# Layer norm in a four-layer network: the first transposition of a norm's tokens also waits for the last of the four normed tiles

## The chip, the cores and the metric

The kernel runs on one core of a Trainium2 chip, as one program with one launch. The metric is the device time in microseconds (us). Each kernel is run several times and the median counts. A profiled execution gives the trace from which the durations and waits below are read.

## The reference

Four layers are applied to `x` of shape (4, 64, 64, 128): four images of 4096 tokens with 128 channels, all in 32-bit floats.

```python
x = L0(x)   # LN -> in_proj -> depthwise 3x3 conv -> four selective scans over 4096 steps
            # (16 states for each of 256 channels) -> LN -> gate -> out_proj; then LN -> MLP
x = L1(x)   # attention over all 4096 positions, softmax over the queries' axis
x = L2(x)   # convolution blocks: 1x1, 3x3, hard swish
x = L3(x)   # LN -> 7x7 neighbourhood attention; then LN -> MLP

def _ln(x, w, b):
    mu = x.mean(-1, keepdims=True)
    var = ((x - mu) ** 2).mean(-1, keepdims=True)
    return (x - mu) * rsqrt(var + 1e-05) * w + b
```

The layer norm stands at four places: ahead of `in_proj` and ahead of the MLP in layer 0, ahead of the attention and ahead of the MLP in layer 3. (The norm ahead of the gate in layer 0 is done in another way and isn't touched.)

## The kernel before, in words

**Work and stages.** Every image goes through the same stages, in chunks of 512 tokens, eight to an image. `scan_inputs` (L283) makes what the scan reads. `selective_scan` (L463) does the recurrence: for each tile GpSimd multiplies `du` with the rows of B (L510, tile `dB`), ScalarE makes exp(delta * A) (L516, `dA`), VectorE scans along the tokens (L518), VectorE or GpSimd multiplies with the rows of C (L523, L531, `hc`), and TensorE sums over the states with a constant matrix `pick` (L564, `py`). `scan_output` (L590), layer 1, layer 2 and `layer3_attention` (L1277) follow; the program calls these together `rest` (L1693). Layer 3's MLP is mixed with the next image's `scan_output`, except for the last image, where `layer3_attention` runs it as `mlp_steps`.

**What runs beside what.** In `network` (L1723) the scan of an image is given a priority number from 10,000,000 on (L1762), and everything else has small numbers, counted up as the program is written. While image 0 is scanned, the `scan_inputs` of images 1 to 3 run in the gaps or ahead of it; while image n is scanned, `rest` of image n-1 runs. After the last scan only `rest` of image 3 is left, with the MLP of image 2 in its first part.

**Who sets the order.** The order of instructions on an engine is not the program's. The framework (`tile.TileContext(nc, schedule_with_timeline_sim=True)`, L1855) plans it when the kernel is built: it keeps its own clock with estimated durations, and at each point gives an engine the instruction with the smallest number among those whose inputs are there by that clock and for which a tile buffer is free. On the chip each engine's queue then has this planned order, and semaphores hold an instruction back where its data comes later than planned. `after` (L88) adds a wait that the data alone would not ask for; its uses in the kernel (L570, L875, L1402 and `Together`, L101) let the first matmul of a group wait for the last of the group's inputs.

**The norm.** `layernorm_T` (L184) handles four tiles of 128 tokens. VectorE makes the statistics (L194, L196), ScalarE the reciprocal deviation (L180, L181), its negative (L198) and four shifts (L200). Then, tile by tile, ScalarE writes the normed tile (L204, `ln_xn`) and TensorE transposes it into a quarter of one PSUM tile (L207). Last, ScalarE reads all four quarters, applies weight and bias, and writes `xnT` (L208), which the next matmuls read. Below, N0 to N3 are the four normed tiles and T0 to T3 the four transpositions. The norm is called 128 times: 32 each in `scan_inputs` (L346), `scan_output` (L662), the attention of layer 3 (L1358) and the MLP of layer 3 (L1315 or L1667). The PSUM tile comes from a pool with four banks in most places; with `wide` (the last image) the attention and the MLP share one buffer for it (L1297).

`everything_again` (L1705), which has further calls, is only run when a bound is exceeded, and the trace shows nothing of it.

Of the kernel before, what the change touches and what calls it, by code (L numbers as in the profile page):

```python
# [87 lines left out]
def after(tc, later, earlier, kind=mybir.DependencyClass.Sync):  # L88
    tc.add_manual_dep(
        later.ins, earlier.ins.name, mybir.DependencyInfo(kind, mybir.DependencyReason.DATA), reason="group"  # L90
    )
# [86 lines left out]
def rstd_of(nc, K, out, var):  # L178

    nc.scalar.activation(out, var, AF.Ln, bias=K.eps)  # L180
    nc.scalar.activation(out, out, AF.Exp, scale=-0.5)  # L181


def layernorm_T(tc, K, pool, psum, x, w, b, out):  # L184


    nc = tc.nc
    stats = pool.tile([128, 4, 6], F32, name="ln_stats", bufs=2)
    mv = pool.tile([128, 4, 2], F32, name="ln_mv", bufs=2)
    rstd = pool.tile([128, 4], F32, name="ln_rstd", bufs=2)  # L190
    less = pool.tile([128, 4], F32, name="ln_less", bufs=2)
    shift = pool.tile([128, 4], F32, name="ln_shift", bufs=2)
    for t in range(4):
        nc.vector.bn_stats(stats[:, t, :], x[:, t, :])  # L194
    for t in range(4):
        nc.vector.bn_aggr(mv[:, t, :], stats[:, t, :])  # L196
    rstd_of(nc, K, rstd, mv[:, :, 1])
    nc.scalar.activation(less, rstd, AF.Copy, scale=-1.0)  # L198
    for t in range(4):
        nc.scalar.activation(shift[:, t : t + 1], mv[:, t, 0:1], AF.Copy, scale=less[:, t : t + 1])  # L200
    xn = pool.tile([128, 4, 128], F32, name="ln_xn", bufs=1)
    pt = psum.tile([128, 4, 128], F32, name="ps")
    for t in range(4):
        nc.scalar.activation(  # L204
            xn[:, t, :], x[:, t, :], AF.Identity, bias=shift[:, t : t + 1], scale=rstd[:, t : t + 1]
        )
        nc.tensor.transpose(pt[:, t, :], xn[:, t, :], K.ident)  # L207
    nc.scalar.activation(out, pt.rearrange("p t c -> p (t c)"), AF.Identity, bias=b, scale=w)  # L208


# [72 lines left out]
def scan_inputs(tc, K, A, D, img):  # L283
# [5 lines left out]
    with ExitStack() as ctx:  # L289
# [50 lines left out]
        for c in range(NCH + 1):  # L340
            acts = []
            if c < NCH:
                xt = pool.tile([128, 4, 128], F32, name="x")
                nc.sync.dma_start(xt, token_tiles(A["x"][img], c))
                xnT = pool.tile([128, LC], F32, name="xnT")
                layernorm_T(tc, K, pool, psum, xt, ln_w, ln_b, xnT)  # L346
                band = pool.tile([128, ND, RC + 2, W], F32, name="band", bufs=3)
                bands[c] = band
                for d in range(ND):
                    ps = psum.tile([128, LC], F32, name="ps")  # L350
                    nc.tensor.matmul(ps, in_proj[:, d * 128 : (d + 1) * 128], xnT, start=True, stop=True)
                    rows = ps.rearrange("p (h w) -> p h w", w=W)
                    nc.scalar.copy(band[:, d, 1 : RC + 1, :], rows)
                    if c > 0:
                        nc.scalar.copy(bands[c - 1][:, d, RC + 1, :], rows[:, 0, :])
                        nc.scalar.copy(band[:, d, 0, :], bands[c - 1][:, d, RC, :])
                sz = pool.tile([128, ND, LC], F32, name="sz")
                for d in range(ND):
                    ps = psum.tile([128, LC], F32, name="ps")
                    mm = nc.tensor.matmul(  # L360
                        ps, in_proj[:, DI + d * 128 : DI + (d + 1) * 128], xnT, start=True, stop=True
                    )
                    if d == 0:
                        together.open(mm)
                    acts.append(lambda d=d, ps=ps, sz=sz: nc.scalar.activation(sz[:, d, :], ps, AF.Silu))
# [224 lines left out]
def scan_output(tc, K, A, D, img, xT, last, scan_over=None):  # L590
# [6 lines left out]
    with ExitStack() as ctx:  # L597
# [17 lines left out]
        def chunk(c, psum=psum, together=together):  # L615
# [44 lines left out]
            yield  # L660
            xnT = pool.tile([128, LC], F32, name="xnT")
            layernorm_T(tc, K, pool, psum, x, ln_w, ln_b, xnT)  # L662
            yield
            po = yield from mlp(tc, K, P, pool, psum, together, xnT, x)
# [612 lines left out]
def layer3_attention(tc, K, A, D, img, wide, out=None):  # L1277
# [7 lines left out]
    with ExitStack() as ctx:  # L1285
# [27 lines left out]
        def mlp_steps(c, x):  # L1313
            xnT = pool.tile([128, LC], F32, name="xnT2", bufs=1)
            layernorm_T(tc, K, pool, made_in, x, n2_w, n2_b, xnT)  # L1315
            yield
            hT = pool.tile([128, NF, LC], F32, name="mlp_h", bufs=1)
            ph = psum.tile([128, NF, LC], F32, name="pair", tag="ps")
            for f in range(NF):
                mm = nc.tensor.matmul(ph[:, f, :], P.w1[:, span(f, 128)], xnT, start=True, stop=True)  # L1320
                if f == 0:
                    together.open(mm)
            together.run(
                mm,
                [
                    lambda f=f: nc.scalar.activation(hT[:, f, :], ph[:, f, :], AF.Gelu, bias=P.b1[:, f : f + 1])  # L1326
                    for f in range(NF)
                ],
            )
            yield  # L1330
            po = fresh((128, LC))
            for f in range(NF):
                nc.tensor.matmul(po, P.w2[:, f, :], hT[:, f, :], start=(f == 0), stop=(f == NF - 1))  # L1333
            yT = pool.tile([128, LC], F32, name="yT", bufs=1)
            nc.scalar.activation(yT, po, AF.Identity, bias=P.b2)  # L1335
            pt = fresh((128, 4, 128))
            for t in range(4):
                nc.tensor.transpose(pt[:, t, :], yT[:, span(t, 128)], K.ident)  # L1338
            nc.vector.tensor_add(x, x, pt)  # L1339
            nc.sync.dma_start(token_tiles(out, c), x)  # L1340
            yield
# [517 lines left out]
```

## Time and profile before

| what | value |
|---|---|
| median of 3 runs | 8721.23 us (8714.47 to 8724.86) |
| the profiled execution | 8724.62 us, its span 8722.7 us, 1.9 us around it |
| TensorE matmuls busy | 7011.5 us (80%) |
| VectorE busy | 7102.0 us (81%) |
| ScalarE busy | 5678.8 us (65%) |
| GpSimd busy | 7121.9 us (82%) |
| mean granted TensorE clock | 0.864 |

The span has three parts. Until about 2000 us the scan of image 0 runs beside `scan_inputs`. From there to about 7700 us the scans of images 1 to 3 run beside `rest` of images 0 to 2. From 7700 us on GpSimd does next to nothing, and `rest` of image 3 runs alone.

How to read the lines: a group's line has the line of the kernel, the engine, the operation, the tiles (output, arrow, inputs), the number of instructions, then busy time and mean duration, then idle time of the engine just ahead of them with what ended it. PE is TensorE's matmuls (a transposition is one), PEld its weight loads, DVE is VectorE, ACT ScalarE, POOL GpSimd, SP SyncE. In a timeline a row has start, duration, engine, line, operation, tiles, count and, in brackets, the idle time ahead of it and who ended it.

### The profile page before, as it was taken

How to read it: one execution, taken by the hardware profiler on the slowest of the kernel's cores; microseconds unless marked ns; L12 is line 12 of the kernel's file. 1: busy time of each engine (PE TensorE's matmuls, PEld its weight loads, DVE VectorE, ACT ScalarE, POOL GpSimd, SP SyncE). 2: the span in 40 equal slices, each digit the busy share in tenths (PEclk: the TensorE clock that was granted, in tenths of full speed). 3: DMA queues.
4: the chain of work that ended last, by engine and by line, in shares of the span. 5: the costliest groups of instructions: out<-in, count | busy, mean ns of one | idle time of the engine just before them, and what ended most of it. 6: DMA issues, size and time to landing. Idle time of an engine off the chain costs nothing. (4 is left out here: it accounts for less than half of the span.)

```text
span 8722.7 us, 102005 instructions
## 1 busy us (share of the span) xinstructions
PE 7011.5 (80%) x30532; PEld 2619.6 (30%) x30532; DVE 7102.0 (81%) x8456; ACT 5678.8 (65%) x11633; POOL 7121.9 (82%) x3111
## 2 busy tenths in 40 slices
PE   6858677686789987777899887777898877888988
PEld 2213122232422222233322222234322222344333
DVE  4788777778999999998899999998899999923433
ACT  5657676665666676667766676667766766654366
POOL 6899989999899989998899989998899999900000
PEclk8768687786899988888899988888999988899989
DMA  5676767677555556565555565565545565620020
GB/s 177 238 256 239 249 224 252 230 246 237 177 175 170 168 170 222 187 222 188 164 174 169 177 202 190 196 224 178 169 167 167 177 211 193 208 73 5 1 83 12
DMA packets 859600, 1562.74 MB, mean 179 GB/s; under 512 B 224389, under 2 KB 342300, under 8 KB 856733
## 3 DMA queue, kind: packets, MB, share of 16 engines
q1 hardware_dynamic: 728733, 1379.93, 48.2%
q10 hardware_dynamic: 130304, 176.19, 5.7%
q8 instruction: 245, 4.01, 0.2%
q14 instruction: 318, 2.61, 0.1%
HBM read 1286.50 MB, written 281.92 MB: 180 GB/s over the span
## 5 line engine op out<-in xcount | busy, mean ns | idle before, releaser
L510 POOL TENSOR_TENSOR dB<-du,b_rows 128x1024 f32<-128x1024 f32 x2048 | 4816.6, 2386 | 405.8 <-DVE hc L518 125.7
L516 ACT ACTIVATE dA<-dt,w_A_log 128x512 f32<-128x512 f32 x4096 | 2777.4, 690 | 482.3 <-DVE hc L518 257.7
L518 DVE TENSOR_TENSOR_SCAN dA<-dA,state,dB 128x512 f32<-128x512 f32 x2072 | 2563.4, 1274 | 289.8 <-POOL dB L510 151.8
L518 DVE TENSOR_TENSOR_SCAN hc<-dA,state,dB 128x512 f32<-128x512 f32 x1512 | 1874.1, 1270 | 303.3 <-ACT dA L516 114.2
L531 POOL TENSOR_TENSOR hc<-hc,c_rows 128x1024 f32<-128x1024 f32 x864 | 2061.9, 2386 | 60.6 <-ACT state L527 18.5
L523 DVE TENSOR_TENSOR hc<-dA,c_rows 128x512 f32<-128x512 f32 x2368 | 1526.0, 678 | 37.8 <-DMA c_rows<-bc_dram 15.2
L564 PE MATMUL py<-hc,pick 128*32 128x512 f32 x8192 | 1242.0, 681 | 266.6 <-POOL hc L531 230.9
L525 ACT COPY state<-dA 128x1 f32<-128x1 f32 x2072 | 319.2, 158 | 1225.5 <-DVE hc L523 1208.6
L854 PE MATMUL pa<-e,l_v 128*128 128x512 f32 x2048 | 1069.4, 654 | 14.9 <-ACT e L810 14.8
L810 ACT ACTIVATE e<-pair 128x1024 f32<-128x1024 f32 (+1 forms) x448 | 509.0, 1136 | 241.3 <-PE pair L806 233.7
L806 PE MATMUL pair<-l_g,l_f 32*128 32x512 f32 x2048 | 527.3, 662 | 169.6 <-ACT e L810 135.4
L854 PEld LDWEIGHTS pa<-e,l_v 128*128 128x128 f32 x2048 | 376.6, 200 | 667.1 <-issue 621.8
L994 POOL MEMSET l_h<- 64x128 f32 x8 | 1.9, 238 | 693.7 <-DVE l_h L968 693.7
L564 PEld LDWEIGHTS py<-hc,pick 128*32 128x32 f32 x8192 | 214.8, 116 | 1019.5 <-issue 476.1
L253 PE MATMUL ps<-band,w_conv_diag 128*128 128x504 f32 (+3 forms) x1152 | 499.0, 592 | 0.0
L1376 PE MATMUL pair<-table,ident 128*128 128x512 f32 x768 | 404.7, 652 | 104.2 <-ACT e L1386 68.7
L207 PE MATMUL ps<-ident,ln_xn 128*128 128x128 f32 x512 | 141.6, 375 | 377.4 <-ACT ln_xn L204 301.1
L518 DVE TENSOR_TENSOR_SCAN dA<-dA,dB 128x512 f32<-128x512 f32 x296 | 348.3, 1212 | 52.5 <-ACT dA L516 28.0
L334 POOL TENSOR_TENSOR du<-delta,xc 128x1024 f32<-128x1024 f32 x128 | 333.5, 2611 | 49.5 <-ACT delta L403 45.1
L1386 ACT ACTIVATE e<-pair 128x1024 f32<-128x1024 f32 (+1 forms) x224 | 254.3, 1135 | 101.4 <-PE pair L1380 100.7
L253 PEld LDWEIGHTS ps<-band,w_conv_diag 128*128 128x128 f32 x1152 | 220.3, 192 | 278.3 <-issue 259.7
L806 PEld LDWEIGHTS pair<-l_g,l_f 32*128 32x128 f32 x2048 | 138.4, 187 | 518.6 <-ACT e L810 266.9
(285 smaller groups left out, 8716.7 us busy)
## 6 DMA issues: line engine op xcount, KB each, us to landing
b_rows<-bc_dram SPq DMA_DIRECT2D x1024, 256.0 KB
c_rows<-bc_dram SPq DMA_DIRECT2D x1024, 256.0 KB
dt<-delta_dram SPq DMA_DIRECT2D x512, 512.0 KB
du<-du_dram SPq DMA_DIRECT2D x512, 512.0 KB
delta_dram<-delta ACTq DMA_DIRECT2D x128, 512.0 KB
du_dram<-du SPq DMA_DIRECT2D x128, 512.0 KB
table<-biasT_dram SPq DMA_DIRECT2D x72, 512.0 KB
y_first_dram<-y_sum ACTq DMA_DIRECT2D x128, 256.0 KB
```

Source lines behind the costliest of these rows:

```text
L253: mm = nc.tensor.matmul(out[:, r0 - row0 : r1 - row0, c0:c1], lhsT((dy + 1) * 3 + dx + 1), src[:, r0 + dy : r1 + dy, c0 + dx : c1 + dx], s ...
L334: nc.gpsimd.tensor_mul(du.rearrange("p d (a b) -> p d a b", b=H), deltas[b].rearrange("p d (a b) -> p d a b", b=H), tk,)
L510: nc.gpsimd.tensor_mul(dB, dus[pp], mid(bt, 2))
L516: nc.scalar.activation(dA, dts[pp][:, g, :], AF.Exp, scale=S.A[:, k, j, pr, g : g + 1])
L518: nc.vector.tensor_tensor_scan(hg[:, order], dA[:, order], dB[:, g, order], 0.0 if i == 0 else state[:, j, pr, g : g + 1], ALU.mult, ALU.add,)
L523: mm = nc.vector.tensor_mul(hc[:, g, :], dA, ct)
L531: made.append(nc.gpsimd.tensor_mul(hc, hc, mid(ct, 2)))
L564: mm = nc.tensor.matmul(py[0][32 * q : 32 * q + 32, :], S.pick, hcs[q // 2][:, q % 2, :], start=(k == 1 and j == 0), stop=(j == NJS - 1),)
L806: nc.tensor.matmul(ps[:, u, :], f[quad, t // 4, span(t % 4, 128)], g[quad, c, :], start=True, stop=True)
L810: made = nc.scalar.activation(e, ps, AF.Exp)
L854: nc.tensor.matmul(pa, v[:, 8 * q + t, :], es[q], start=(t == 0 and q == 0), stop=(t == 7 and q == 3),)
L1376: nc.tensor.matmul(ps[:, u, :], K.ident, t[:, u, :], start=True, stop=False)
```

## The change

The loop that normed a tile and transposed it becomes two loops: first all four normed tiles, then all four transpositions. T0 gets an added wait for N3, the last normed tile. No instruction is added or removed, and the arithmetic is the same. All four call sites get it.

```diff
     xn = pool.tile([128, 4, 128], F32, name="ln_xn", bufs=1)
     pt = psum.tile([128, 4, 128], F32, name="ps")
     for t in range(4):
-        nc.scalar.activation(
+        normed = nc.scalar.activation(
             xn[:, t, :], x[:, t, :], AF.Identity, bias=shift[:, t : t + 1], scale=rstd[:, t : t + 1]
         )
-        nc.tensor.transpose(pt[:, t, :], xn[:, t, :], K.ident)
+    for t in range(4):
+        turned = nc.tensor.transpose(pt[:, t, :], xn[:, t, :], K.ident)
+        if t == 0:
+            after(tc, turned, normed)
     nc.scalar.activation(out, pt.rearrange("p t c -> p (t c)"), AF.Identity, bias=b, scale=w)
```

## The prediction

> **What bounds the kernel now.** I read five views: the busy time by stretches, the waits of VectorE and GpSimd, the instructions on the tile `ln_xn`, the timeline around single norms, and the chain that ended last. First the stretches (length; busy us and count of PE, PEld, DVE, ACT, POOL; granted clock, DMA share, GB/s):
>
> ```profile
> 0.00:2000.00 2000.00, 1427.71 (x4420) 500.28 (x4420) 1493.55 (x1786) 1305.42 (x2953) 1775.62 (x795) 0.77 0.69 236
> 2000.00:7700.00 5700.00, 4696.83 (x21744) 1715.78 (x21745) 5257.22 (x6135) 3818.51 (x7856) 5345.48 (x2313) 0.88 0.57 186
> 7700.00:7920.00 220.00, 192.66 (x754) 111.76 (x753) 40.84 (x166) 145.98 (x301) 0.00 (x0) 0.95 0.15 45
> 7920.00:8420.00 500.00, 452.61 (x1761) 177.71 (x1760) 204.86 (x192) 205.12 (x198) 0.80 (x4) 0.96 0.04 11
> 8420.00:8722.70 302.70, 241.66 (x1856) 114.07 (x1856) 105.50 (x178) 203.73 (x329) 0.00 (x0) 0.90 0.14 51
> ```
>
> Up to 7700 us GpSimd is the bound: 7121.1 of 7700 us, idle 578.9, with VectorE close by (92% from 2000 us on) and TensorE at 82%. Behind 7700 us TensorE is: 886.9 of 1022.7 us, idle 135.8. So a wait of TensorE counts fully in the last part, and before it only where VectorE or GpSimd then wait for TensorE. Those waits, up to 7700 us (engine, line, releaser: us, times, longest):
>
> ```profile
> DVE hc L518 <- PE py L564: 122.3, 30, 11.2
> ...
> POOL dB L510 <- DVE hc L518: 125.7, 59, 8.1
> POOL dB L510 <- PE py L564: 53.2, 14, 9.2
> ```
>
> The tile that the change touches, over the whole span (who TensorE waited for ahead of T0 to T3, then who waited for them):
>
> ```profile
> L207 PE MATMUL ps<-ident,ln_xn x512: 272/421/477, 20.7 to 8701.6; 128*128 128x128 f32 x171
> ...
>   ACT ln_xn L204: 656.6, 189
> ...
>   ACT xnT L208: 22.5, 17
> ...
>   POOL hc L531: 7.7, 3
>   POOL dB L510: 2.2, 3
> ```
>
> 656.6 us counts the weight loads and the matmuls of the same stalls; by the matmul rows alone it is 301.1 (74 gaps over 1 us ahead of a transposition, of all releasers, sum to 369). Does the scan pay for it? I took every idle stretch over 1 us of VectorE or GpSimd up to 7700 us that TensorE ended (253 us together) and looked whether a gap over 1 us ahead of T0 lay in the 18 us before it. That holds for four of them, 9.1 us in sum. Most of the rest lies before 2000 us, where the transpositions start 6 to 45 us after their inputs are there. So the scan hardly pays for T0's wait today.
>
> **What the change does to one norm.** In the timeline I sorted the 128 norms by when T0 started against N3's end.
>
> - *Ready*, 69 norms: T0 started after N3 had ended. The added wait is met; directly nothing changes.
> - *Follow*, 31 norms (4 in the first part, 21 beside the later scans, 6 behind 7700): T0 to T3 each ran as their tile came.
> - *Split*, 28 norms (23 and 5): T0 ran at once, then 2 to 44 other matmuls, then T1 to T3.
>
> One of each of the last two, TensorE alone:
>
> ```profile
> 8700.47 1.63 PE L207 MATMUL ps<-ident,ln_xn 128*128 128x128 f32 x4 [4.04 <-ACT ln_xn L204]
> ```
> ```profile
> 7882.14 0.47 PE L207 MATMUL ps<-ident,ln_xn 128*128 128x128 f32 x1 [6.47 <-ACT ln_xn L204]
> 7882.41 6.17 PE L239 MATMUL ps<-mlp_h,w_fc_w 128*128 128x512 f32 x8
> 7888.41 1.05 PE L242 MATMUL ps<-ident,x 128*128 128x128 f32 x8
> 7889.30 0.49 PE L207 MATMUL ps<-ident,ln_xn 128*128 128x128 f32 x3
> ```
>
> *Price of a follow.* T0 must wait 1.15 to 1.77 us longer, for three more normed tiles (0.39 us apart, more where something lies between). Then four transpositions run without a gap: 0.66 us at a high clock (the four of L1338 at 8713.80), 1.11 at a low one (the four at 2161.02). Before, only T3 (0.27 to 0.48) came behind N3. So `xnT`, and all that is queued behind T3, comes 0.66 − 0.27 = 0.4 to 1.11 − 0.48 = 0.6 us later. Queued behind T3 are mostly eight `pick` matmuls of the scan, and on ScalarE, behind `xnT`, the next exponentials (L516). In all at most 31 × 0.6 = 19 us. Of these the 6 behind 7700 us, at 0.4 to 0.6, are sure: 2.4 to 3.6 us (the last norm stands in the chain that ended last). The 25 others, 15 us, lie beside the scan; by the 9 of 253 us above they would be worth half a microsecond, if VectorE and GpSimd were hit in full 15.
>
> *Price of a split.* What stood between T0 and T1 was waiting behind T0 and not for it. With T0's readiness put off to N3, the planner can place it ahead of T0. In the example above TensorE stood for 6.47 us with the MLP's second product behind it, whose inputs (L232, done by 7878.1) were there; that stall is filled, and T0 to T3 come together. Before 7700 us this is hidden, as shown. Behind it there are five: stalls of 6.5 and 2.8 us with long work behind, 3.5 us with only two matmuls behind (kept), and two without a stall. Gain: up to 9.3 us, at least nothing.
>
> *PSUM.* The tile is taken at T0, so it is taken later: by 1.2 us in a follow, by up to 9 in a split. This frees a bank for others, or lets another tile go ahead of it where there is one buffer. No row prices it; both signs belong to the order, below.
>
> *The clock: a rule against the change.* Row: granted clock 0.77, 0.88 and 0.90 to 0.96 in the stretches; four transpositions take 1.11 or 0.66 us with it. The Trainium skill (TensorE: Matmul & The Clock Gate, "Why this matters for your kernels") says that idle gaps beyond about 3 us between bursts throw the array back to half its clock. The added wait lifts gaps of 2 to 3.4 us over that mark: three among the follows and splits (2.7, 2.3 and 2.8 us). By the rule each costs one such time at half speed, an estimate of 1.7 us of work, so 5 us; by the row nothing is sure, since the stalls of 6 to 13 us that already stand there left the clock of 2000 to 7700 us at 0.88. I take 2.
>
> *The order.* This is the part that the trace can't price. In at least 59 norms T0's place in the plan moves, and with it which instruction each engine takes next. A bound: how much does the pace of the scan differ when other work lies beside it? In the five stretches of 1000 us from 2000 to 7000 GpSimd was busy for 942.2, 942.9, 941.9, 941.0 and 947.7 us, so the pace keeps within 0.5% of their mean, 943.1. Over 7700 us that is ± 38 us. In the last part a tenth of TensorE's idle time, chosen as no row is near, is ± 14. From both sides: −52 to +52, more if a stage's buffers get tangled.
>
> **Sum.** Against the profiled execution's 8724.6 us (span 8722.7 and 1.9 around it), and carried over to the median of 8721.2: follows +2.4 to +19, splits −9.3 to 0, clock 0 to +5, order −52 to +52. Known parts alone: −7 to +24.
>
> **The rivals.**
>
> *A, slower (0.47).* The follows' lateness reaches the scan. ScalarE waits at `xnT` with exponentials queued behind it; VectorE's idle time already has 288 us that exponentials ended, so it has no cushion there. All 19 us count; the splits' gain is lost again, because the matmuls put ahead of T0 come late themselves in places; clock +2, order +3. 8721 + 24 = 8745. For it: what is to be won is limited (9 us behind T0 in the scan, 9.3 in the last part), while a plan whose stalls are hidden at present can mainly lose. Case from 8739 to 8820.
>
> *B, no change (0.30).* The scan hides the follows, and the last part's +3 and −9 nearly cancel: 8715 to 8721. For it: 69 norms are untouched, and the 9 us above. It fails only by the order.
>
> *C, faster (0.23), the other side.* One mechanism: work that stood behind T0 goes ahead. Place: the splits of `scan_output` beside the scan and in the last part. Price: the stalls ahead of T0 in the 28 splits and a few like them sum to about 135 us. It decides from the point where the freed matmuls release `hc` tiles or the next image's chain; if a fifth of the 135 us gets through, that is 27 us: 8694. For it: from the start of those stalls up to 7700 us to 6 us behind T0, 273 us in sum, GpSimd was idle for 61, where its mean would give 17. Against it: VectorE, which shares the bound, was idle for 34 where its mean gives 21, and only 9 us of all that idle time was ended by TensorE; the norm's own work on VectorE and ScalarE in those places takes the scan's turn too, and stays. Case from 8660 to 8703.
>
> That the wait doesn't bind is case B too: if the planner kept every order and N3 were early, the time would be 8721.
>
> A is likeliest, so 8745. The range reaches over B and most of C and A: 8682 to 8815. The measurement can tell about 0.2% (17 us) from no change; by the cases: faster 0.23, same 0.30, slower 0.47.
>
> **What would show it.** In the profile after, splits should be gone: T0 to T3 back to back, and TensorE's wait on `ln_xn` in fewer and longer gaps. A shows as more idle time of VectorE ended by exponentials and of GpSimd ended by L518, with the stretch before 7700 longer. B: the same 7700 and a last part within 10 us. C: less idle of GpSimd up to 7700, or the MLP stretch at 7700 to 7920 shorter by 9 us or more. I'd be wrong in kind if the time moved by over 1%: then the planner's order, not the wait, made the time.

## The result and the profile after

The median is 8777.29 us (8772.18 to 8789.84, six runs) against 8721.67 us of six runs of the kernel before: a ratio of 1.0066, with an interval of 1.0056 to 1.0077. That is 56 us slower, where 24 were predicted. The profiled execution took 8778.09 us, its span 8776.4 us. Of the line numbers in the kernel after, those from L207 on are three higher than before (`ln_xn` is transposed at L208 now; the exponentials stand at L519, the scans at L521).

The busy time by stretches, as in the prediction (the last one ends later):

```profile
0.00:2000.00 2000.00, 1421.89 (x4444) 499.41 (x4444) 1495.73 (x1791) 1310.02 (x2965) 1783.03 (x798) 0.77 0.69 236
2000.00:7700.00 5700.00, 4639.28 (x21553) 1706.98 (x21552) 5227.21 (x6099) 3791.84 (x7804) 5336.40 (x2310) 0.88 0.56 185
7700.00:7920.00 220.00, 191.03 (x828) 115.15 (x828) 44.40 (x167) 131.56 (x278) 0.00 (x0) 0.93 0.23 71
7920.00:8420.00 500.00, 453.94 (x1730) 180.06 (x1728) 194.29 (x185) 218.56 (x229) 0.79 (x4) 0.96 0.01 3
8420.00:8776.40 356.40, 276.58 (x1988) 127.66 (x1984) 121.72 (x216) 221.34 (x358) 0.00 (x0) 0.89 0.16 56
```

This view tells little. GpSimd, which the prediction took for the bound, has done as much by 7700 us as before (7119.4 us against 7121.1), so the scan is not 50 us late; and yet everything behind 7700 us is. The granted clocks are the old ones within 0.02.

The waits of VectorE and GpSimd, up to 7662 us, where the scan now ends; ahead of them, from before, the two that the prediction did not show:

```profile
DVE dA L518 <- ACT dA L516: 148.5, 114, 5.6
DVE hc L518 <- ACT dA L516: 139.9, 105, 6.0
```
```profile
DVE hc L521 <- ACT dA L519: 153.7, 111, 5.8
DVE dA L521 <- ACT dA L519: 153.3, 119, 5.7
DVE hc L521 <- PE py L567: 106.9, 28, 11.2
...
POOL dB L513 <- DVE hc L521: 133.2, 66, 11.1
...
POOL dB L513 <- PE py L567: 50.1, 14, 9.1
```

The two waits for exponentials come to 307.0 us (before 288.4), the two for TensorE have become shorter by 15.4 and 3.1 us, GpSimd's for the scan is longer by 7.5. The tile `ln_xn`:

```profile
L208 PE MATMUL ps<-ident,ln_xn x512: 272/421/477, 21.7 to 8755.9; 128*128 128x128 f32 x171
...
  ACT ln_xn L204: 549.6, 83
  ACT state L528: 294.5, 34
...
  PEld ps L208: 284.0, 42
  PE ps L208: 265.6, 41
```

By the row of `ln_xn`, 549.6 us where there were 656.6, TensorE would seem to wait less. It waits more. The row of L528, 294.5 us where before had 9.9, is in the main the same wait under another name: 15 of these stalls of the matmuls, 136.6 us, end 0.05 us behind N3. Counted directly, as stalls of T0 to T3 that end within 0.12 us of the end of a normed tile, they come to 402.2 us in 56 (before 301.6 in 65). So the wait is in the trace as it was meant, in fewer and longer stalls, and it is 100 us larger. The transposition itself is what it was. Two norms of the timeline, TensorE alone: the one that was the prediction's example of a split, and the last one:

```profile
7931.35 1.12 PE L208 MATMUL ps<-ident,ln_xn 128*128 128x128 f32 x4 [7.80 <-ACT ln_xn L204]
7932.26 4.51 PE L242 MATMUL ps<-mlp_h,w_fc_w 128*128 128x512 f32 x8
...
8755.22 1.11 PE L208 MATMUL ps<-ident,ln_xn 128*128 128x128 f32 x4 [5.18 <-ACT ln_xn L204]
```

The split is gone, as in all 28 places. But the stall ahead of it is still there, 7.80 us instead of 6.47: the second product of the MLP was not put ahead of the norm. And the last norm waits 1.14 us longer (5.18 against 4.04) and then saves 0.52 us of it.

**Where the 56 us are.** The next two views cut the span where VectorE's last scan instruction ends, and where TensorE's last matmul of layer 3's attention of image 2 ends (L1413, L1416 after). Before, then after:

```profile
0.00:7647.30 7647.30, 6086.85 (x25972) 2196.63 (x25974) 6740.19 (x7888) 5105.74 (x10767) 7121.00 (x3107) 0.85 0.60 199
7647.30:7664.80 17.50, 15.36 (x86) 4.73 (x82) 1.81 (x3) 4.88 (x6) 0.10 (x1) 1.00 0.08 23
7664.80:8722.70 1057.90, 909.26 (x4476) 418.24 (x4476) 359.96 (x566) 568.13 (x860) 0.80 (x4) 0.93 0.11 35
```
```profile
0.00:7662.00 7662.00, 6025.41 (x25742) 2190.76 (x25744) 6720.55 (x7886) 5091.86 (x10757) 7119.43 (x3107) 0.85 0.59 199
7662.00:7717.20 55.20, 49.57 (x318) 20.49 (x314) 3.07 (x5) 14.29 (x16) 0.00 (x0) 0.99 0.13 41
7717.20:8776.40 1059.20, 907.74 (x4476) 418.01 (x4476) 359.72 (x566) 567.16 (x860) 0.79 (x4) 0.93 0.11 35
```

The last part has the same instructions and the same length (1057.9, 1059.2). The scan ends 14.6 us later. The rest of the loss is the middle row: attention that is not done when the scan is done. It was 17.5 us before and is 55.2 now, and nothing hides it. In before's timeline, VectorE's end of that stretch with its first instruction of image 3's `rest`, and what TensorE does then:

```profile
7647.15 1.27 DVE L523 TENSOR_TENSOR hc<-dA,c_rows 128x512 f32<-128x512 f32 x2
7662.87 0.69 DVE L1409 TENSOR_TENSOR oT<-rec,po 128x512 f32<-128x512 f32 x1 [14.44 <-ACT rec L1407]
7664.80 0.69 DVE L1415 TENSOR_TENSOR x<-x,pj 128x512 f32<-128x512 f32 x1 [1.25 <-PE pj L1413]
7667.87 0.27 DVE L609 MEMSET center<- 128x256 f32 x1 [2.37 <-DMA x_dram<-x]
```
```profile
7663.61 1.16 PE L1413 MATMUL pj<-w_proj_w,oT 128*128 128x128 f32 x8 [0.27 <-DVE oT L1409]
7677.66 6.21 PE L627 MATMUL ps<-y,center 128*128 128x512 f32 x8 [12.90 <-DMA y<-y_dram]
```

So already before, the scan was not the last to end. The chain of `rest` was: `scan_output`, layer 1, layer 2 and the attention of images 0, 1 and 2, one behind the other. Image 3's own `rest` waits for its end: the row of L609 starts when the attention's last tile has been written to memory (`x_dram<-x`), and TensorE goes on 13 us behind the attention (12 after).

### The profile page after: what moved, and what is told of

Read it like the earlier page. It is cut to its first block, busy times and chain, and to the rows that moved or that the text cites. A ratio compares the mean times of both kernels' runs of the same rounds, so it can differ in the third digit from the quotient of the medians.

```text
span 8776.4 us, 102009 instructions
## 1 busy us (share of the span) xinstructions
PE 6982.7 (80%) x30532; PEld 2629.3 (30%) x30532; DVE 7083.3 (81%) x8456; ACT 5673.3 (65%) x11633; POOL 7120.2 (81%) x3111
## 5 line engine op out<-in xcount | busy, mean ns | idle before, releaser
L519 ACT ACTIVATE dA<-dt,w_A_log 128x512 f32<-128x512 f32 x4096 | 2777.8, 690 | 540.7 <-DVE hc L521 285.1
L521 DVE TENSOR_TENSOR_SCAN dA<-dA,state,dB 128x512 f32<-128x512 f32 x2072 | 2559.0, 1272 | 305.3 <-POOL dB L513 145.1
L521 DVE TENSOR_TENSOR_SCAN hc<-dA,state,dB 128x512 f32<-128x512 f32 x1512 | 1872.4, 1267 | 293.3 <-ACT dA L519 120.6
L567 PE MATMUL py<-hc,pick 128*32 128x512 f32 x8192 | 1221.9, 673 | 243.8 <-POOL hc L534 204.1
L528 ACT COPY state<-dA 128x1 f32<-128x1 f32 x2072 | 318.8, 158 | 1203.2 <-DVE hc L526 1184.8
L208 PE MATMUL ps<-ident,ln_xn 128*128 128x128 f32 x512 | 119.9, 378 | 466.6 <-ACT ln_xn L204 265.6
L521 DVE TENSOR_TENSOR_SCAN dA<-dA,dB 128x512 f32<-128x512 f32 x296 | 348.2, 1212 | 49.0 <-ACT dA L519 25.8
```

What stands on the lines that cost most here:

```text
L519: nc.scalar.activation(dA, dts[pp][:, g, :], AF.Exp, scale=S.A[:, k, j, pr, g : g + 1])
L521: nc.vector.tensor_tensor_scan(hg[:, order], dA[:, order], dB[:, g, order], 0.0 if i == 0 else state[:, j, pr, g : g + 1], ALU.mult, ALU.add,)
L567: mm = nc.tensor.matmul(py[0][32 * q : 32 * q + 32, :], S.pick, hcs[q // 2][:, q % 2, :], start=(k == 1 and j == 0), stop=(j == NJS - 1),)
```

## Experiments

Three theories go through what follows. *A* is the prediction's case: each norm's lateness reaches the scan by ScalarE and VectorE. *W*: the added wait itself costs, in proportion to how long it is and in how many norms it stands. *P*: the wait costs next to nothing on the chip; the planner, which knows of it, puts the whole program in another order, and in that order the chain of `rest` lies further back among the scan's instructions. The first four expectations call *P* by the letter *O*. The edits are shown by their main lines.

### A third of the wait, and the wait by places

T0 waits for N1 instead of N3:

```diff
-            after(tc, turned, normed)
+            after(tc, turned, normed[1])   # normed is a list here
```

> T0 waits for the second normed tile N1 instead of the fourth, at all four places: a third of the added wait (about 0.4 us a norm instead of 1.2). Theory W (the wait itself lengthens the chain of the rest stages, which ends about 17 us behind the scan before and so sets when the last image's part can start): about a third of the loss, +15 to +25 us, 8737 to 8747. Theory O (the wait only makes the planner sort anew, and the time is what that order happens to give): no third; anywhere from -40 to +60, as likely below 8721 as above.

Measured: 8771.22 us, 1.0063 (1.0046 to 1.0080) of the kernel before, which took 8720.73 beside this kernel and the next three. A third of the wait gives nine tenths of the loss. So W's proportion to the length of the wait is wrong.

Then the full wait in one place at a time, with a flag that the call sites set:

```diff
-        if t == 0:
+        if t == 0 and K.grouped:
             after(tc, turned, normed)
```

In `scan_output` (L662) and in layer 3's MLP (L1667), which is mixed with it (56 norms; the expectation says 64, but eight MLP norms are the last image's, L1315):

> The change only in the norms of layer 0's second half and of layer 3's MLP beside it (64 of 128 norms, those that were split most), the other norms as before. Theory W: nearly the whole loss, since the stages with these norms grew by 18, 26 and 4 us in the changed kernel: +40 to +56, 8762 to 8778. Theory O: a new order again, so a number of its own, from -20 to +80.

In the attention of layer 3, and in the MLP of the last image:

> The change only in the norms ahead of layer 3's attention, and in the last image's MLP (40 norms). Theory W: 0 to +8 us (32 norms by 0.2 on the chain, and the last image's +4), 8721 to 8729. Theory O: a new order beside the last two thirds of the kernel, -30 to +50, and the three places don't add up to the +56 of the whole.

In `scan_inputs`:

> The change only in the norms of scan_inputs (32 norms, 28 of which had their wait met in any case). Theory W: the changed kernel was 8 us ahead after this part, so -8 to 0, 8713 to 8721; the planned order of all that follows must come out almost as before. Theory O: if the order of what follows is sorted anew too, any number from -30 to +50.

Measured: `scan_output` with MLP 8772.03 us, 1.0064 (1.0047 to 1.0081); attention 8725.34, 1.0005 (0.9997 to 1.0014); `scan_inputs` 8716.98, 0.9998 (0.9989 to 1.0006). The differences of 51, 5 and −4 us sum to 52, so the places add up, and one of them makes the loss. In the `scan_inputs` kernel ScalarE, VectorE and GpSimd have exactly the order of before, and TensorE too, but for two neighbouring matmuls. So it shows the wait without another order, and it costs nothing; but it is a weak test, since in 28 of its 32 norms T0 started behind N3 in any case. The attention kernel is a better one. In before, T0 ran ahead of N3's end in 20 of the 24 attention norms beside the scan; all of these are held back here, and the cost is 5 us (−3 to +12).

The kernel of `scan_output` also decides between A and P. Its stretches, cut at the same two events as above:

```profile
0.00:7628.30 7628.30, 6014.44 (x25630) 2176.31 (x25630) 6726.61 (x7886) 5092.70 (x10753) 7117.94 (x3107) 0.85 0.59 199
7628.30:7703.70 75.40, 67.35 (x434) 28.20 (x426) 3.21 (x5) 18.96 (x21) 0.00 (x0) 0.99 0.19 64
7703.70:8770.00 1066.30, 919.19 (x4476) 421.78 (x4476) 359.68 (x566) 567.37 (x860) 0.79 (x4) 0.92 0.11 35
```

Its scan ends 19.0 us earlier than before, and the kernel is 51 us slower. By A it would be the other way round. The chain of `rest` ends 38.9 us later, and the last part takes 8.4 us more.

**Plan or chip?** An engine runs its queue in the planned order: all 11633 instructions of ScalarE come in the same order in before's trace and in that of the `scan_inputs` kernel. So the place of a stage's end among the 4096 exponentials of the scan, in ScalarE's queue, is the plan's doing; the pace at which that queue moves shows what the chip makes of it. The end of layer 2 of image 2 (its last matmul on TensorE), in the rows of the exponentials up to that moment, is a point where both can be read. Before, after, and the `scan_output` kernel:

```profile
L516 ACT ACTIVATE dA<-dt,w_A_log x3742: 666/692/777, 97.6 to 7054.9; 128x512 f32<-128x512 f32 x197
```
```profile
L519 ACT ACTIVATE dA<-dt,w_A_log x3769: 666/692/774, 98.3 to 7105.2; 128x512 f32<-128x512 f32 x199
```
```profile
L520 ACT ACTIVATE dA<-dt,w_A_log x3788: 664/692/806, 97.0 to 7108.3; 128x512 f32<-128x512 f32 x200
```

The same counts for the kernels so far and two that follow, from each trace (in us; the scan ends with VectorE's last scan instruction, the attention of image 2 with its last matmul):

| kernel | exponentials ahead of it | layer 2 ends | us for one | scan ends | attention ends |
|---|---|---|---|---|---|
| before | 3742 | 7055.6 | 1.8855 | 7647.3 | 7664.8 |
| after | 3769 | 7105.5 | 1.8853 | 7661.8 | 7717.2 |
| T0 waits for N1 | 3767 | 7109.4 | 1.8873 | 7657.6 | 7704.2 |
| `scan_output` | 3788 | 7109.8 | 1.8769 | 7628.3 | 7703.7 |
| attention | 3742 | 7050.8 | 1.8842 | 7641.9 | 7660.7 |
| T1 waits for N3 (below) | 3739 | 7050.7 | 1.8857 | 7648.4 | 7674.3 |
| short norm (below) | 3748 | 7126.2 | 1.9013 | 7736.8 | 7756.1 |

How far do such figures move by themselves? Three kernels keep ScalarE's order of before up to the last part (`scan_inputs`, and below the last part alone and the short norm there). In their traces layer 2 ends at 7049.8, 7052.4 and 7047.5 us, at 1.8833 to 1.8847 us for one, and the attention at 7657.9, 7665.9 and 7654.0. So up to some 12 us between two rows say nothing; the 50 us of the slow versions do.

After, 27 more exponentials stand ahead, and 27 × 1.885 is 51 us; layer 2 ends 49.9 us later. The pace is the same to one part in a thousand, though TensorE stood 100 us longer at the norms. If the wait slowed the chip, the pace would have moved. (That a wait's cost and an order's gain cancel there can't be excluded by this alone; the attention kernel speaks against it.) In the three slow versions of the wait the count is what makes the loss. In the `scan_output` kernel the pace moved too, the other way: its 46 more would be 87 us, and a faster pace took 33 of them back. Nor do they get there in the same way: after has 10 more by the end of image 0's `scan_output`, 25 by that of image 1 and 25 by that of image 2; with the wait for N1 it is 0, −2 and 17, and 30 by the end of layer 1 of image 2. The loss is like in size by chance more than by rule.

### Less work in the chain of rest

If `rest` is the bound, then with less of it the loss should go. These two leave out the last of eight chunks of layer 1's attention for images 0 to 2 (its tokens keep their input), without and with the change:

```diff
-        for c in range(NCH):
+        for c in range(NCH if wide else NCH - 1):
```

> The kernel before with the last of the eight chunks of layer 1's attention left out for images 0 to 2 (its 512 tokens keep their input), so that the stages beside the scan are shorter by some 70 us an image. Theory P (the time is made by the chain of the rest stages, which the plan puts among the scan's exponentials, and which before ends 17 us after the scan): now the scan ends last, at about 7640, and the last part of 1052 us follows: about 8690 to 8700, no more than 30 below the kernel before, although over 200 us of chain are gone. Theory A (the scan pays for the norm's wait): the same here; the pair with the next run tells them apart.

> The changed kernel with the same chunk left out. In its planned order of ScalarE 3979 of the 4096 exponentials stand ahead of the end of image 2's layer 3, against 3963 in the run before: both well ahead of the scan's end. Theory P: the loss of 56 us shrinks to what the scan and the last part differ by, 0 to +20 against the light kernel before. Theory A or W (the wait costs time wherever it stands): 40 to 56 us against the light kernel before.

Measured: without the change 8715.08 us, 0.9993 (0.9985 to 1.0002) of the 8723.69 of before; with it 8688.38, 0.9957 (0.9943 to 0.9971). The change isn't slower here; it is 27 us faster. With the change, cut where the attention of image 2 ends and where the scan ends (now in this order):

```profile
0.00:7444.80 7444.80, 5863.52 (x25168) 2133.14 (x25168) 6550.97 (x7693) 4977.06 (x10532) 6925.76 (x3025) 0.85 0.60 201
7444.80:7644.80 200.00, 88.60 (x325) 24.28 (x324) 194.18 (x211) 95.17 (x210) 190.47 (x83) 0.59 0.55 183
7644.80:8687.10 1042.30, 900.20 (x4432) 410.06 (x4428) 352.37 (x539) 560.99 (x837) 1.68 (x5) 0.93 0.09 30
```

The chain is through 200 us ahead of the scan, and now the scan ends last. With the chain off the path, the loss is gone. That speaks against a wait that costs time wherever it stands; a cost in the chain alone, which is W in the sense of the first run, is not touched by this pair. Both numbers missed P's forecast, though. P had the kernel without the change at 8690 to 8700: its scan ended at 7676.4 us, 29 later than in before, though less work lay beside it. And P had the pair 0 to 20 us apart, the changed one behind: its scan ended 31.5 us earlier and its last part took 6.4 us longer. Another order moves the scan by that much too, in either direction, and no run here says why.

### The wait at T1 instead of T0

```diff
-        if t == 0:
+        if t == 1:
```

> T0 goes as before as soon as its tile is there, and T1 waits for N3 instead, at all four places: the last three transpositions, and xnT behind them, are put off just as in the change, only T0 is not. In the planned order 3741 exponentials of the scan stand ahead of the end of image 2's layer 2, where the kernel before has 3742 and the changed one 3769. Theory P: the time goes with that count, so no change, 8715 to 8730. Theory W (later transpositions cost the time): most of the loss, 8750 to 8775.

Measured: 8739.78 us, 1.0022 (1.0012 to 1.0032). That lies between the two, in neither's range. The same normed tiles are waited for, by three transpositions of four, and three tenths of the loss are left. The count, in the table, is before's within three, so P gives nothing for these 16 us. The trace can't place them: the profiled run, 8731 us, was the fastest of nine, and it shows layer 2 ending 4.9 us earlier, the attention 9.6 us later and a last part 2.9 us shorter, all within what such figures move by themselves.

### A shorter norm

If a norm's lateness cost time, a shorter norm should gain. Five instructions on ScalarE become one on VectorE:

```diff
-    nc.scalar.activation(less, rstd, AF.Copy, scale=-1.0)
-    for t in range(4):
-        nc.scalar.activation(shift[:, t : t + 1], mv[:, t, 0:1], AF.Copy, scale=less[:, t : t + 1])
+    nc.vector.scalar_tensor_tensor(shift, mv[:, :, 0], -1.0, rstd, ALU.mult, ALU.mult)
```

> The kernel before with the five small ScalarE instructions that make the norm's shift replaced by one of VectorE, 1.06 us less on ScalarE in each of 128 norms. The count ahead of the end of image 2's layer 2 is 3748, so 6 more than before. Theory P: the chain beside the scan is 6 exponentials later, +7 to +10 us, and the last part, where nothing else fills the gap, is shorter by 0.8 us in each norm on its chain, -8 to -15: 8710 to 8725. Theory A (ScalarE's lateness reaches the scan, so relief of ScalarE is relief of the scan): faster by 50 us or more, below 8675.

Measured: 8800.90 us, 1.0095 (1.0078 to 1.0112). P and A were both wrong. The rows of `ln_shift` show where the norm became slower (who its engine waited for, then who waited for it):

```profile
L197 DVE SCALAR_TENSOR_TENSOR ln_shift<-ln_mv,ln_rstd x128: 122/164/9159, 19.0 to 8767.8; 128x4 f32<-128x4 f32 x128
...
  ACT ln_rstd L181: 46.3, 40
...
  PEld ps L204: 484.7, 130
  PE ps L204: 430.5, 52
  ACT ln_xn L201: 133.5, 36
```

An instruction of 164 ns, but it stands in VectorE's queue among scans of 1.27 us, and ScalarE waits for it 133.5 us in all. In the 24 attention norms beside the scan, the time from the start of the reciprocal deviation to N3 went from 4.26 to 8.29 us in the mean. Here the pace falls, as the table shows: 6 more exponentials are worth 11 us, and 3748 × (1.9013 − 1.8855) is 59. This is how a lateness on the chip would look in these numbers, and after has none of it; but the order is another here too, and how much of the 59 us is the order's doing isn't shown.

In this kernel the last part took 1034.8 us, against 1057.9. So the edit was tried there alone:

```diff
+    K.short = wide     # around the calls of rest; wide is the last image
```

> The kernel before with the norm's shift made by one VectorE instruction, but only in the last part (32 norms), where VectorE has idle time. In the run with this in all norms the last part took 1028 us instead of 1052, and the parts beside the scan lost 90. Theory P: beside the scan nothing changes, and the last part is 15 to 24 us shorter: 8697 to 8707, faster than both kernels. If the last part's gain there came from its other order, less: 8710 to 8721.

Measured: 8701.09 us, 0.9978 (0.9968 to 0.9987) of the 8721.77 us of before beside it. That is 21 us faster than before and so faster than both kernels, in P's range. In its trace the last part took 1046.4 us, 11.5 less than before, where P had 15 to 24; the other 10.8 us lie ahead of it, where the order is before's. ScalarE at the last norm, before and with this edit:

```profile
8698.94 0.20 ACT L198 ACTIVATE ln_less<-ln_rstd 128x4 f32<-128x4 f32 x1
8699.18 0.85 ACT L200 ACTIVATE ln_shift<-ln_mv,ln_less 128x1 f32<-128x1 f32 x4
8699.94 1.63 ACT L204 ACTIVATE ln_xn<-x,ln_shift,ln_rstd 128x128 f32<-128x128 f32 x4
```
```profile
8674.75 0.20 ACT L181 ACTIVATE ln_rstd<-ln_rstd 128x4 f32<-128x4 f32 x1
8675.19 1.65 ACT L208 ACTIVATE ln_xn<-x,ln_shift,ln_rstd 128x128 f32<-128x128 f32 x4 [0.23 <-DVE ln_shift L200]
```

With VectorE idle, the hop costs a gap of 0.23 us and replaces about 1 us of work. Beside the scan, the same hop cost several.

### The last part, and the MLP

The change in the last part's 32 norms alone (the flag is set for the last image), with the order of before up to there:

> The change only in the norms of the last part (rest of image 3 and the MLP of image 2, 32 norms); the planned order up to there is that of the kernel before, so this is the part that stands alone behind the scan. Prediction's terms: follows +2.4 to +3.6, splits -9.3 to 0. From the changed kernel's own trace, where the last part took 1053.2 us against 1051.8: +1, so 8718 to 8727. A loss of 20 us or more here would mean that the 56 us are not made beside the scan.

And in L1667's MLP alone, to part it from `scan_output` (24 norms; the expectation says 32):

> The change only in the norms of layer 3's MLP that run beside scan_output (32 norms, images 0 to 2 and no others). The count of exponentials planned ahead of the end of image 2's layer 2 is that of the kernel before, 3742. Theory P: no change, 8715 to 8730, which leaves the loss to the 32 norms of scan_output. Theory W: a share of the loss as these norms have a share of the splits, +15 to +25.

Measured: last part 8729.17 us, 1.0007 (0.9998 to 1.0015); MLP 8724.02, 1.0004 (0.9995 to 1.0012). With the places above, what is left is the 24 norms of `scan_output` for images 0 to 2: they make the loss, alone or together with the MLP that is mixed with them. No run has them alone.

## Why the prediction was right in sign and wrong in path

The sign was right by luck, and so was the range. The forecast of +24 us was 19 from follows that reach the scan, 2 from the clock and 3 from the order; what cost the time was the order, with some 50.

**The bound.** The step that failed: "a wait of TensorE counts fully in the last part, and before it only where VectorE or GpSimd then wait for TensorE". It was read from shares of busy time. Two streams share the engines up to 7700 us, and the end of the scan was taken for the end of the stretch because its engine is the busiest. The other stream ended 17.5 us later, and the timeline around 7650 us, which the prediction did not look at, shows it: VectorE with a gap of 14.44 us, TensorE at attention. What puts that stream back counts in full, as long as it ends last.

**Case A's path.** Of the signs it named, VectorE's waits for exponentials grew by 19 us and GpSimd's for the scan by 7.5, and the scan ended 14.6 us later. Those would not have cost 56, and in the `scan_output` kernel the scan was earlier and the loss was there. A is refuted as the cause.

**The order.** The term is mis-sized, and it is nearly everything. It stood in the sum with +3 and a bound of ±52, from the scan's pace. The bound held for the scan (+14.6; −19 in the `scan_output` kernel, +29 in the light one). What moved was the place of the other stream in the queues: 27 exponentials, 50 us. That this is inside ±52 is chance, since the scan's pace doesn't bound such a shift. The text said that a move of over 1% would show the order at work; it took 0.66%.

**The follows.** The price of 0.4 to 0.6 us was good: the attention norms beside the scan took 10.70 us from the start of the statistics to `xnT`, on average, after 10.05. In `scan_output` and its MLP, 40 norms beside the scan, the whole norm even became shorter, 25.40 us after 27.30 on average: T0 to T3 took 0.97 us instead of 3.87, for a T0 that came 2.0 us later behind N3. So the place that makes the loss is one where the norm itself is faster, which speaks against W once more.

**The splits.** All gone, as predicted, but nothing was gained in the last part: TensorE's waits there for `ln_xn` went from 28.8 us in 7 to 37.4 in 10. The change in the last part alone gave +7 us (−2 to +13); the prediction's terms for that part, follows and splits, came to −7 to +4.

**The clock.** The prediction held the mean of 0.88 beside the later scans against the rule on idle gaps. But the granted clock in these traces is either 1.0 or 0.5, so 0.88 means 23% of that time at half. In before, 88 stalls of TensorE of 3 us or more began at 1.0, and 87 of them were followed by 0.5 within 3.6 us of their end; that agrees with the rule, which the Trainium skill (TensorE: Matmul & The Clock Gate, "Why this matters for your kernels") gives as no idle gaps beyond about 3 us. Shorter stalls were followed by it too, 67 of 80 of 2 to 3 us; for a moment at 1.0 picked at random it is about a quarter within 6 us. With the change the time at half grew from 2373 to 2438 us. In the last part, where TensorE's time counts, the mean was 0.93 in both, so a cost of 0 to 5 us can't be told from nothing here.

**The rivals.** C's mechanism, work going ahead of T0, is not in the norm that was its best example: the stall of 6.47 us is one of 7.80. And TensorE's stalls at the norms, which C wanted filled, grew by 100 us. B describes `scan_inputs`, attention and MLP well (−4 to +5 us), and fails "only by the order", as it said.

**What stays open.** The wait in `scan_output` with the order of before was not tried, since the order follows from the wait; that it would cost little there rests on the pace and on the attention kernel. The 16 us of the wait at T1 have no cause yet, as they come without more exponentials ahead. Why the planner's order with this wait puts more of the scan ahead of `rest` isn't settled either. Some of the loss comes behind `scan_output`: from layer 1 on to the end of its attention image 2 took 1478 us before and 1491 after.

## What to carry to other kernels

Where two streams share in-order queues, find out which of them ends last before a stretch is called bound by the busiest engine: look at the few microseconds in which the stretch ends. When a planner sets the order, an added wait is first an input to the plan; count in the new queue how much of the other stream stands ahead of each stage's end, times that stream's pace. That gave 51 us here where 50 were measured; but 87 for 54 where the pace moved too, and nothing for the 16 us of T1, so it is a first reading and not the sum. A step that is cheap on an idle engine (0.23 us of waiting here) can cost several microseconds behind a busy one's queue (the way from the reciprocal deviation to N3 grew from 4.26 to 8.29 us), so an edit may be right in one stage and wrong in another.

## What the runs showed of the hardware

The pace of the interleaved queues hardly depends on their order: 1.877 to 1.887 us for one of the scan's exponentials of 0.69 us, over 7000 us, in six of the seven kernels of the table. That TensorE stood 100 us longer at the norms with the change (402.2 us in 56 stalls, before 301.6 in 65) didn't move it. In the kernel with a 164 ns instruction per norm in VectorE's queue it was 0.8% slower.

The granted clock is 1.0 or 0.5, nothing between. In before, a transposition of 128x128 in 32-bit floats took 272 to 333 ns in the stretches at 1.0 and 417 to 477 ns in those at 0.5 (by the profile, which models a matmul's end).
